# Turning layer 1's softmax shift with one 32-column transpose and eight small DMAs

## The chip, the cores and the metric

The kernel runs on one core of a Trainium2 chip. Its time is the device time of one execution in microseconds (us). The median of three runs counts. One further execution was recorded by the hardware profiler.

## What is computed

Two transformer layers act on `x` of 2048 tokens by 128 channels, each with a modulated layer norm before attention and before a feed-forward part. The change is in the attention of layer 1, which has 8 query heads of 16 channels, one shared key and value head, and a causal mask:

```python
h = _layernorm(x, axis=-1) * (1 + ca) + sa
k = h @ Wk
v = h @ Wv
q = jnp.einsum('btc,qcd->bqtd', h, Wq)
wei = jnp.einsum('bqtd,bsd->bqts', q, k) * scale
wei = jnp.where(causal, wei, -jnp.inf)
wei = jax.nn.softmax(wei, axis=-1)
out = jnp.einsum('bqts,bsd->btqd', wei, v).reshape(b, t, -1)
x = x + ga * (out @ Wp + bp)
```

Layer 0 has attention over all 2048 keys with 16 heads of 8 channels, then a mixture of 16 experts with one chosen per token. Layer 1 ends in a feed-forward part that mixes each token with the one before it.

## The kernel before, in words

One function, `attention`, serves both layers. `fused` is true in layer 0 and false in layer 1. The queries lie in four blocks `b` of 512 (`QB`), the heads in groups `grp` of four. A unit is one pair (b, grp), so layer 1 has eight units, numbered 0 to 7 in the order of blocks: units 0 and 1 belong to block 0, units 6 and 7 to block 3. In layer 1 a unit of block b sees only the keys of blocks 0 to b.

Each unit runs in two passes:

- The first pass (`first_pass`, the step's matmul at L381) computes scores with the queries on the partitions, and VectorE takes the largest per query and head: L385 for whole key blocks, L390 for the block that the mask crosses. Its ending, `largest`, writes the negated maxima into a tile `nm`, as a rounded part (L408) and a remainder (L409).
- The turn (`turn`) brings these maxima from one query per partition to one query per column. TensorE transposes `nm` into a PSUM bank and ScalarE copies the result into a tile `mT`.
- The second pass (`second_pass`) computes the scores again with the keys on the partitions (`score`, L458). In layer 1 a second matmul adds the shift to the same PSUM tile: a matrix of ones against `shift[u]` (L464). ScalarE takes the exponential (L468), GpSimd clears what the mask forbids (L471), and TensorE multiplies by the values (`weigh`, L484).

In layer 0 the shift needs no matmul of its own, because the rows of `mT` are sent by DMA into free rows of the stacked queries `qS` (L424). There `nm` has 32 columns, and one transpose (L417) and one copy of 32 rows (L419) turn it. In layer 1 the shift is a tile `mT` of 128 rows by 512 columns in which, for each of the two row groups of 64, four rows hold numbers and the rest are zero. To get them, `nm` is a zeroed tile of 128 by 512 in which eight columns per 128 are written, and four transposes of 128 by 128 (L431) and a copy of 128 by 512 (L432) turn it.

Three things set the order of the work. First, the program order: `look_ahead` runs the first pass ahead of the second by up to `LEAD` = 8 steps, and calls a unit's `turn` on the third call after its maxima are done. Second, a planner reorders each engine's instructions by its own estimate of when their operands are ready; it may place instructions of different units among each other, on SyncE's queue too. Third, each engine then works strictly in its order. Score tiles of both passes share three PSUM buffers (`ps_s`), and two further banks hold the weighted sums (`av`) and serve everything else (`other_bank`).

The ending of a unit (`normalise`) copies the weighted sum (L554), transposes it back (L522), divides (L526, L527), and after the second group of a block transposes again (L534), copies (L537), projects (L543) and adds to `x` (L550). The queries of block b + 1 are prepared during the first passes of block b: `project_q` splits them and `stack` (L260) sends them by sixteen DMAs of 64 KB, all on SyncE's queue, into `qS`. The next norm's statistics (L180, L181) and the finished rows of the output (L1247) are also made in these gaps.

Of the kernel before, what the change touches and what calls it, by code (L numbers as in the profile page):

```python
# [10 lines left out]
F32 = mybir.dt.float32  # L11
F32R = mybir.dt.float32r
# [7 lines left out]
P = 128  # L20
T = 2048
NT = T // P
QB = 512
NB = T // QB
TB = QB // P
# [9 lines left out]
RT = 64  # L35
# [8 lines left out]
def two_layers(ctx: ExitStack, tc: tile.TileContext, a: dict, out: bass.AP):  # L44
    nc = tc.nc
# [3 lines left out]
    ident = const.tile([P, P], F32, name="ident")  # L49
# [237 lines left out]
    def attention(layer, hT, ngrp, dk, scale, causal, kvp, begin, prepare, wq, bq, folded, ended,  # L287
# [16 lines left out]
        L = f"a{layer}"  # L304
        step = RT // dk
        fused = step > 4
        lag = int(causal)
        S = P // RT
        nst = HG // S
        nrow = S * dk  # L310
        with ExitStack() as s:
            qp = s.enter_context(tc.tile_pool(name=L + "q", bufs=2))
# [9 lines left out]
            def other_bank():  # L322
                nonlocal others
                others += 1
                return banks[(weighing + 1 if fused or weighing >= 0 else others) % 2]
# [4 lines left out]
            qS = {}  # L330
# [4 lines left out]
                ones = kvp.tile([P, nst, P], F32R, name=L + "ones")  # L335
                nc.gpsimd.tensor_copy(ones, ones_rows.unsqueeze(2).to_broadcast([P, nst, P]))
            masked = kvp.tile([P, QB], F32, name=L + "masked") if causal else None
            negmax = []
            for i in range(2):
                shape = [P, nst, TB, S, 2] if fused else [P, TB, P]  # L340
                t = kvp.tile(shape, F32, name=f"{L}nm{i}", tag=f"nm{i}")
                nc.gpsimd.memset(t, 0.0)
                negmax.append(t)

            units = [(b, grp) for b in range(NB) for grp in range(ngrp)]
            attended = {}
# [21 lines left out]
            def first_pass(u):  # L368

                b, grp = units[u]  # L370
                pm = qp.tile([P, TB, HG, NB], F32, name=f"{L}mx{u}", tag="mx")
                nkb = b + 1 if causal else NB

                def step(i, kb, pair):
                    own = causal and kb == b
                    n = (i + 1) * P if own else QB
                    ps = ps_s.tile([P, 2, QB], F32, name=f"{L}p1_{u}_{i}_{kb}_{pair}", tag="s")
                    for j in range(2):
                        g = 2 * pair + j
                        st, r = grp * nst + g // S, RT * (g % S)  # L380
                        nc.tensor.matmul(ps[:, j, :n], qS[b][r:r + RT, st, i * P:(i + 1) * P],  # L381
                                         kS(st)[r:r + RT, kb * QB:kb * QB + n],
                                         start=True, stop=True)
                    if not own:
                        nc.vector.tensor_reduce(pm[:, i, 2 * pair:2 * pair + 2, kb], ps,  # L385
                                                AX.X, ALU.max)
                    for j in range(2 if own else 0):

                        g = 2 * pair + j
                        nc.vector.tensor_tensor_reduce(  # L390
                            masked[:, :n], ps[:, j, :n], later[:, QB - n:], 1.0, LOWEST,
                            ALU.add, ALU.max, pm[:, i, g, kb:kb + 1])

                def largest():
                    nx = qp.tile([P, TB, HG], F32, name=f"{L}nx{u}", tag="nx")
                    nc.vector.tensor_reduce(nx, pm[:, :, :, :nkb], AX.X, ALU.max, negate=True)
                    nm = negmax[u % 2]
                    if fused:


                        parts = [(nm[:, k],
                                  nx[:, :, k * S:(k + 1) * S]) for k in range(nst)]
                    else:

                        parts = [(nm.rearrange("p t (g w) -> p t g w", w=RT)[:, :, :, 2 * k:],
                                  nx[:, :, k * S:(k + 1) * S]) for k in range(nst)]
                    for v, nk in parts:
                        nc.vector.tensor_copy(v[:, :, :, 0].bitcast(F32R), nk)  # L408
                        nc.vector.tensor_tensor(v[:, :, :, 1], nk, v[:, :, :, 0], ALU.subtract)  # L409

                def turn():
                    nm = negmax[u % 2]
                    ps = other_bank()
                    if fused:
                        n = nst * TB * 2 * S
                        mT = qp.tile([n, P], F32R, name=f"{L}mT{u}", tag="mT")
                        nc.tensor.transpose(ps[:n, :P], nm.rearrange("p k t g w -> p (k t g w)"),  # L417
                                            ident)
                        nc.scalar.copy(mT, ps[:n, :P])  # L419

                        for k in reversed(range(nst)):
                            for i in range(TB):
                                r = (k * TB + i) * 2 * S
                                nc.sync.dma_start(  # L424
                                    out=qS[b][31::32, grp * nst + k,
                                              i * P:(i + 1) * P].bitcast(F32),
                                    in_=mT[r:r + 2 * S, :].bitcast(F32))
                    else:
                        mT = qp.tile([P, QB], F32R, name=f"{L}mT{u}", tag="mT")
                        for i in range(TB):  # L430
                            nc.tensor.transpose(ps[:, i * P:(i + 1) * P], nm[:, i, :], ident)  # L431
                        nc.scalar.copy(mT, ps)  # L432
                    shift[u] = mT

                steps = [(lambda i=i, kb=kb, pair=pair: step(i, kb, pair))
                         for i in range(TB) for kb in range(nkb) for pair in range(HG // 2)]
                last = steps.pop()
                return steps + [lambda: (last(), largest(), turns.append([0, turn]))]

            def second_pass(u):  # L440
# [429 lines left out]
    def last0(late, bank, ps_s, ep):  # L870
# [41 lines left out]
        def rows():  # L912
# [8 lines left out]
                lambda: tiles(lambda k: (times(k), down(k))), add]  # L921

    attention(0, hT, H0 // HG, D0, 1.0 / math.sqrt(D0), False, pool, begin0, None, wq0,
              vcol(V_BQ), [], ended0, last0,
              [lambda n=n: clear(n) for n in range((NE + 1) * T // (P * CLEAR))])
# [17 lines left out]
    with ExitStack() as s:  # L943
# [147 lines left out]
        for t in range(NT):  # L1091
            nc.gpsimd.indirect_dma_start(
                out=yx[:, t, :], out_offset=None, in_=a["y_rows"],
# [185 lines left out]
    def last1(late, bank, ps_s, ep):  # L1279
# [9 lines left out]
        def begin():  # L1289
# [8 lines left out]
                       lambda: b.square(nc.vector), lambda: b.value(banks[2], 2)]  # L1298

    attention(1, h2, H1 // HG, D1, float(P) ** -0.5, True, pool1,  # L1300
              lambda ep, pp, stacks: ((lambda st: kS1), (lambda kt, head: vA1[:, kt, :]), qS1),
              ready1, wq1, None, folded1, early, last1)
# [66 lines left out]
```

## Time and profile before

| | before |
|---|---|
| median of three runs | 1236.22 us (1233.09 to 1239.17) |
| profiled execution: own time, span | 1246.91 us, 1245.2 us |
| PE (matmul) busy | 1146.1 us, 92% of the span |
| DVE busy | 953.1 us, 77% |
| ACT busy | 766.6 us, 62% |
| POOL busy | 85.0 us, 7% |
| mean DMA rate | 36 GB/s |

PE is TensorE's matmul, PEld its weight load, DVE VectorE, ACT ScalarE, POOL GpSimd, and SPq the queue from which SyncE issues DMAs. Busy shares are averages over the whole span; the attention of layer 1 is the stretch from about 935 to 1222 us. "Granted clock" is the share of full speed that TensorE was given. In rows of one line the three numbers with slashes are the least, the median and the longest duration in ns, and `out<-in` names what is written and read.

### The profile page before, as it was taken

What the parts mean: (1) busy time and instruction counts of PE and PEld (TensorE: products, weight loads), DVE (VectorE), ACT (ScalarE), POOL (GpSimd) and SP (SyncE); (2) the same over time, 40 slices, a digit from 0 to 9 for tenths busy, and PEclk for the clock granted to TensorE, in tenths of its full rate; (3) what the DMA queues carried; (4) which work ended last, traced back from release to release, by engine and by line L of the source; (5) the groups of instructions that cost most, each with busy time, mean ns of one, the idle gap of its engine ahead of it and who ended that gap; (6) DMA issues with size and microseconds to landing.
All of it is one profiled execution on the core that took longest, in us unless ns stands there. A gap on an engine that the chain in (4) does not pass through costs nothing.

```text
span 1245.2 us, 22565 instructions
## 1 busy us (share of the span) xinstructions
PE 1146.1 (92%) x9216; PEld 519.8 (42%) x9216; DVE 953.1 (77%) x1550; ACT 766.6 (62%) x845; POOL 85.0 (7%) x152
## 2 busy tenths in 40 slices
PE   4579999999999999999999999979858999999995
PEld 2233333334433443343343343447624444444443
DVE  4788898899889889889989883343458688898532
ACT  6107777777777777777777778643323355556763
POOL 2002000000000000000000000320321011100101
PEclk9658999999999999999999999999967789999997
DMA  4841010212220212110000000033210101000000
GB/s 125 113 50 35 2 51 3 70 28 77 70 70 2 69 39 79 56 53 2 1 2 2 2 2 2 20 118 91 64 30 15 35 1 35 1 1 1 2 22 13
DMA packets 63880, 45.23 MB, mean 36 GB/s; under 512 B 7009, under 2 KB 57825, under 8 KB 63265
## 3 DMA queue, kind: packets, MB, share of 16 engines
q1 hardware_dynamic: 61008, 40.37, 13.2%
q10 hardware_dynamic: 1744, 1.32, 0.6%
q0 software_dynamic: 1024, 2.10, 0.6%
q8 instruction: 73, 1.20, 0.4%
q14 instruction: 31, 0.25, 0.1%
HBM read 9.88 MB, written 21.95 MB: 26 GB/s over the span
## 4 chain that ended last, share of the span: by engine, by line
PE 80%; DVE 12%; ACT 4%; DMA 1%; issue 1%; another core or an unknown queue 1%; DVEq 0%; SPq 0%; ACTq 0%; POOLq 0%; POOL 0%
PE a0bank L484 24%; PE a0p L458 17%; PE a0p L381 13%; PE a1bank L484 5%; PE a1p L458 4%; DVE a0mx L385 3%; DVE a1mx L385 3%; PE a1p L381 2%; PE a1p L464 2%; DVE a1masked L390 2%; PE sg L987 2%; ACT a0e L468 1%; PE gu L1039 1%; PE a0bank L522 1%
## 5 line engine op out<-in xcount | busy, mean ns | idle before, releaser
L385 DVE TENSOR_REDUCE a0mx<-a0p 128x2 f32<-128x1024 f32 x512 | 623.9, 1225 | 71.3 <-PE a0p L381 61.4
L468 ACT ACTIVATE a0e<-a0p 128x1024 f32<-128x1024 f32 x512 | 521.8, 1024 | 178.7 <-PE a0p L458 154.1
L484 PE MATMUL a0bank<-a0e,vA 128*32 128x256 f32 x4096 | 333.2, 391 | 1.7 <-ACT a0e L468 1.7
L381 PE MATMUL a0p<-kS,a0qS 64*128 64x512 f32 x1024 | 248.2, 480 | 26.4 <-DVE a0mx L385 13.1
L458 PE MATMUL a0p<-a0qS,kS 64*128 64x512 f32 x1024 | 260.5, 497 | 0.0
L468 ACT ACTIVATE a1e<-a1p 128x1024 f32<-128x1024 f32 (+3 forms) x160 | 143.1, 896 | 109.8 <-PE a1p L464 106.6
L458 PEld LDWEIGHTS a0p<-a0qS,kS 64*128 64x128 f32 x1024 | 97.2, 184 | 204.4 <-issue 132.2
L381 PEld LDWEIGHTS a0p<-kS,a0qS 64*128 64x128 f32 x1024 | 100.2, 192 | 111.4 <-ACT a0e L468 57.1
L484 PEld LDWEIGHTS a0bank<-a0e,vA 128*32 128x32 f32 x4096 | 86.3, 108 | 137.8 <-issue 121.5
L385 DVE TENSOR_REDUCE a1mx<-a1p 128x2 f32<-128x1024 f32 x96 | 115.8, 1221 | 14.5 <-PE a1p L381 13.7
L484 PE MATMUL a1bank<-a1e,vA 128*32 128x256 f32 (+1 forms) x1152 | 97.1, 386 | 0.4 <-POOL a1e L471 0.4
L458 PE MATMUL a1p<-a1qS,kS 64*128 64x512 f32 (+3 forms) x320 | 77.7, 470 | 5.2 <-DVE a1mx L385 3.9
L381 PE MATMUL a1p<-kS,a1qS 64*128 64x512 f32 (+3 forms) x320 | 68.2, 426 | 11.4 <-DVE a1mx L390 5.1
L390 DVE CUSTOM_DVE_ANT_0 a1masked<-a1p,later 128x128 f32<-128x128 f32 (+3 forms) x128 | 62.4, 488 | 10.6 <-PE a1p L381 5.2
L793 POOL DMA_INDIRECT sent<-hs,row_i x16 | 16.0, 999 | 707.6 <-DVE ln11xn L229 684.0
L464 PE MATMUL a1p<-a1mT,a1ones 64*128 64x512 f32 (+3 forms) x320 | 62.5, 379 | 0.0
L458 PEld LDWEIGHTS a1p<-a1qS,kS 64*128 64x128 f32 x320 | 32.0, 191 | 63.8 <-issue 25.5
L381 PEld LDWEIGHTS a1p<-kS,a1qS 64*128 64x128 f32 x320 | 33.1, 201 | 38.5 <-DVE a1mx L390 12.7
L484 PEld LDWEIGHTS a1bank<-a1e,vA 128*32 128x32 f32 x1152 | 25.7, 109 | 42.6 <-issue 35.3
L471 POOL TENSOR_SCALAR_AFFINE_SELECT a1e<-a1e 128x256 f32<-128x256 f32 x64 | 26.0, 407 | 234.7 <-ACT a1e L468 234.7
L464 PEld LDWEIGHTS a1p<-a1mT,a1ones 64*128 64x128 f32 x320 | 32.5, 195 | 1.7 <-issue 1.3
L419 ACT CAST a0mT<-a0bank 32x128 fp32r<-32x128 f32 x16 | 4.0, 253 | 41.2 <-PE a0bank L417 41.2
(384 smaller groups left out, 698.7 us busy)
## 6 DMA issues: line engine op xcount, KB each, us to landing
sent<-blank SPq DMA_DIRECT2D x68, 256.0 KB
kS<-a0qS SPq DMA_DIRECT2D x28, 128.0 KB
a0qS<-a0mT SPq DMA_DIRECT2D x128, 2.0 KB
wgu_sb<-in_gate_up SPq DMA_DIRECT2D x1, 2048.0 KB
a0qS<-a0qh SPq DMA_DIRECT2D x62, 32.0 KB
a0qS<-a0ql SPq DMA_DIRECT2D x62, 32.0 KB
xs<-sent SPq DMA_DIRECT2D x31, 64.0 KB
y_rows<-y SPq DMA_DIRECT2D x7, 256.0 KB
```

The costliest lines, as they stand in the source:

```text
L381: nc.tensor.matmul(ps[:, j, :n], qS[b][r:r + RT, st, i * P:(i + 1) * P], kS(st)[r:r + RT, kb * QB:kb * QB + n], start=True, stop=True)
L385: nc.vector.tensor_reduce(pm[:, i, 2 * pair:2 * pair + 2, kb], ps, AX.X, ALU.max)
L390: nc.vector.tensor_tensor_reduce(masked[:, :n], ps[:, j, :n], later[:, QB - n:], 1.0, LOWEST, ALU.add, ALU.max, pm[:, i, g, kb:kb + 1])
L458: nc.tensor.matmul(ps[:, j, q0:], kS(st)[r:r + RT, kt * P:(kt + 1) * P], qS[b][r:r + RT, st, q0:], start=True, stop=fused)
L464: nc.tensor.matmul(ps[:, j, q0:], ones[r:r + RT, g // S, :], shift[u][r:r + RT, q0:], start=False, stop=True)
L468: nc.scalar.activation(e[:, :, q0:], ps[:, :, q0:], AF.Exp, scale=scale)
L471: nc.gpsimd.affine_select(out=e[:, :, q0:q0 + P], in_=e[:, :, q0:q0 + P], compare_op=ALU.is_ge, fill=0.0, base=0, pattern=[[0, 2], [1, P]] ...
L484: nc.tensor.matmul(av[g * W:(g + 1) * W, c0:c1], vA(kt, grp * HG + g), held[kt, g // 2][:, g % 2, c0:c1], start=(kt == 0 and c0 == 0), sto ...
L522: nc.tensor.transpose(ps[:, i * P:(i + 1) * P], o[:, i * P:(i + 1) * P], ident)
L793: nc.gpsimd.indirect_dma_start(out=sent[t], in_=hs[:, i, :], in_offset=None, out_offset=bass.IndirectOffsetOnAxis(ap=row_i.bitcast(U32)[:, ...
L987: nc.tensor.matmul(ps[:, j, :], w[:, k * P:(k + 1) * P], hT[:, b * QB:(b + 1) * QB], start=True, stop=True)
L1039: nc.tensor.matmul(ps[:, i, :], xsT[q][:, i * P:(i + 1) * P], wgu[:, bass.ds(regs[j], 1), :].rearrange("p a f -> p (a f)"), start=True, st ...
```

## The change

In layer 1 the maxima of every unit but unit 0 now go into a tile `nm` of 32 columns, ordered by row group, query tile, pair and part. The turn of these units is one transpose of 32 columns (now L422) and one copy of 32 rows into `small` (L424). Then eight DMAs of four rows by 128 columns (2 KB each, L433) on SyncE's queue put the rows into one of two tiles `rows_of`, at rows 0 to 3 and 64 to 67. These two tiles take the part of `mT` in turn. The second of them is zeroed once by GpSimd; the first is written whole by unit 0, which keeps the four wide transposes through the tile `wide`. The tiles `nm` are no longer zeroed in either layer, since all their columns are written. Lines after the change stand seven further down from `second_pass` on (L458 is L465, L464 is L471, L484 is L491); the first pass's L381 is L383.

```diff
--- before.py
+++ after.py
@@ -335,12 +335,14 @@
                 ones = kvp.tile([P, nst, P], F32R, name=L + "ones")
                 nc.gpsimd.tensor_copy(ones, ones_rows.unsqueeze(2).to_broadcast([P, nst, P]))
             masked = kvp.tile([P, QB], F32, name=L + "masked") if causal else None
-            negmax = []
-            for i in range(2):
-                shape = [P, nst, TB, S, 2] if fused else [P, TB, P]
-                t = kvp.tile(shape, F32, name=f"{L}nm{i}", tag=f"nm{i}")
-                nc.gpsimd.memset(t, 0.0)
-                negmax.append(t)
+            negmax = [kvp.tile([P, nst, TB, S, 2] if fused else [P, S, TB, nst, 2], F32,
+                               name=f"{L}nm{i}", tag=f"nm{i}") for i in range(2)]
+            if not fused:
+
+                wide = kvp.tile([P, TB, P], F32, name=L + "wide")
+                nc.gpsimd.memset(wide, 0.0)
+                rows_of = [kvp.tile([P, QB], F32R, name=f"{L}rows{i}") for i in range(2)]
+                nc.gpsimd.memset(rows_of[1].bitcast(F32), 0.0)
 
             units = [(b, grp) for b in range(NB) for grp in range(ngrp)]
             attended = {}
@@ -400,9 +402,12 @@
 
                         parts = [(nm[:, k],
                                   nx[:, :, k * S:(k + 1) * S]) for k in range(nst)]
+                    elif u:
+                        parts = [(nm[:, :, :, k].rearrange("p g t w -> p t g w"),
+                                  nx[:, :, k * S:(k + 1) * S]) for k in range(nst)]
                     else:
 
-                        parts = [(nm.rearrange("p t (g w) -> p t g w", w=RT)[:, :, :, 2 * k:],
+                        parts = [(wide.rearrange("p t (g w) -> p t g w", w=RT)[:, :, :, 2 * k:],
                                   nx[:, :, k * S:(k + 1) * S]) for k in range(nst)]
                     for v, nk in parts:
                         nc.vector.tensor_copy(v[:, :, :, 0].bitcast(F32R), nk)
@@ -411,25 +416,27 @@
                 def turn():
                     nm = negmax[u % 2]
                     ps = other_bank()
-                    if fused:
-                        n = nst * TB * 2 * S
-                        mT = qp.tile([n, P], F32R, name=f"{L}mT{u}", tag="mT")
-                        nc.tensor.transpose(ps[:n, :P], nm.rearrange("p k t g w -> p (k t g w)"),
-                                            ident)
-                        nc.scalar.copy(mT, ps[:n, :P])
-
-                        for k in reversed(range(nst)):
+                    n = nst * TB * 2 * S
+                    if fused or u:
+                        small = qp.tile([n, P], F32R, name=f"{L}mT{u}", tag="mT")
+                        nc.tensor.transpose(
+                            ps[:n, :P], nm.rearrange("p a t b w -> p (a t b w)"), ident)
+                        nc.scalar.copy(small, ps[:n, :P])
+                        for c in reversed(range(nst if fused else S)):
                             for i in range(TB):
-                                r = (k * TB + i) * 2 * S
-                                nc.sync.dma_start(
-                                    out=qS[b][31::32, grp * nst + k,
-                                              i * P:(i + 1) * P].bitcast(F32),
-                                    in_=mT[r:r + 2 * S, :].bitcast(F32))
+                                cols = slice(i * P, (i + 1) * P)
+                                r = (c * TB + i) * 4
+                                if fused:
+                                    dst = qS[b][31::32, grp * nst + c, cols]
+                                else:
+                                    dst = rows_of[u % 2][c * RT:c * RT + 4, cols]
+                                nc.sync.dma_start(out=dst.bitcast(F32),
+                                                  in_=small[r:r + 4, :].bitcast(F32))
                     else:
-                        mT = qp.tile([P, QB], F32R, name=f"{L}mT{u}", tag="mT")
                         for i in range(TB):
-                            nc.tensor.transpose(ps[:, i * P:(i + 1) * P], nm[:, i, :], ident)
-                        nc.scalar.copy(mT, ps)
+                            nc.tensor.transpose(ps[:, i * P:(i + 1) * P], wide[:, i, :], ident)
+                        nc.scalar.copy(rows_of[0], ps)
+                    mT = None if fused else rows_of[u % 2]
                     shift[u] = mT
 
                 steps = [(lambda i=i, kb=kb, pair=pair: step(i, kb, pair))
```

## The prediction

> **What bounds the kernel now.** I read the page's busy shares first, then stage windows, then the rows around the "turn" of layer 1, unit by unit. The change touches attention layer 1 only, which runs from about 935 to 1222 us of the 1245.2 us span. In the stage windows (columns: window, its length, then busy us and count for PE, PEld, DVE, ACT, POOL, then granted TensorE clock, DMA share, GB/s):
>
> ```profile
> 1030.00:1045.00 15.00, 13.96 (x134) 6.73 (x134) 14.11 (x29) 6.64 (x9) 2.44 (x6) 1.00 0.01 2
> 1045.00:1061.00 16.00, 15.41 (x133) 7.77 (x132) 13.12 (x25) 10.85 (x14) 0.81 (x2) 1.00 0.26 67
> 1061.00:1077.00 16.00, 14.15 (x132) 6.30 (x131) 15.12 (x51) 9.64 (x10) 0.51 (x2) 1.00 0.00 1
> 1077.00:1100.00 23.00, 22.71 (x217) 10.97 (x216) 19.87 (x32) 13.74 (x17) 2.75 (x7) 1.00 0.01 2
> ```
>
> PE is the bound in most of it (96% and 99% busy in the second and fourth row); DVE leads where a unit's maxima end (14.11 of 15, 15.12 of 16), and ACT never does. So PE time removed counts, and a PE stall counts almost in full. What the change works on:
>
> ```profile
> L431 PE MATMUL a1bank<-ident,a1nm x32: 272/273/477, 935.4 to 1165.3; 128*128 128x128 f32 x32
> ...
> L432 ACT CAST a1mT<-a1bank x8: 581/586/587, 936.6 to 1165.9; 128x512 fp32r<-128x512 f32 x8
> ```
>
> And the form that layer 0 already uses, which layer 1 now gets:
>
> ```profile
> L417 PE MATMUL a0bank<-ident,a0nm x16: 270/284/393, 83.6 to 758.0; 128*32 128x128 f32 x16
> ...
> L419 ACT CAST a0mT<-a0bank x16: 239/254/255, 84.0 to 758.5; 32x128 fp32r<-32x128 f32 x16
> ...
> L424 SPq DMA_DIRECT2D a0qS<-a0mT x128: 497/497/594, 84.3 to 762.7; - x128
> ```
>
> **What it takes away.** Seven units lose three of four transposes each. Four in a row span 0.66 us at full clock (1044.05, below), one 0.27: 0.38 saved; at half clock (unit 2: 978.12 to 979.24) 0.84. Only where nothing else sets the unit's start does this reach the end: units 2, 3, 5, 7 give 0.84 + 3 x 0.38 = 2.0 us. Seven ACT copies get shorter by 586 - 254 = 332 ns (2.3 us), but ACT has at least 30% idle in each window above: worth 0, or 2.3 at most. The DVE writes stay four per unit of 0.17 us, and POOL's two 128x512 memsets (0.52 each) are two again: 0; layer 0 only loses two small memsets, and its PE order is unchanged: 0.
>
> **What it adds.** 7 x 8 = 56 DMAs on SP, and a wait: the first ones-matmul (L464 before, L471 now) of a unit now waits for eight landings instead of one ACT copy. PE works in order, so behind it wait all scores, and through the three PSUM score tiles DVE's maxima and ACT's exponentials. The price of the path is read from layer 0, which has the same eight 2 KB DMAs:
>
> ```profile
> 757.95 0.28 PE L417 MATMUL a0bank<-ident,a0nm 128*32 128x128 f32 x1
> ...
> 758.49 0.24 ACT L419 CAST a0mT<-a0bank 32x128 fp32r<-32x128 f32 x1
> ...
> 758.76 4.47 SPq L424 DMA_DIRECT2D a0qS<-a0mT  x8
> ```
>
> 0.78 us from transpose to end of copy, 4.47 for eight issues, and the last issue (762.73) is followed by its last packet 1.24 us after it began (in the unit before: issue 718.75, packets to 719.99). That is 0.75 + 7 x 0.57 + 1.25 = 6.0 us from the transpose to a ready shift; before it was 1.28. Here a rule speaks against a small number: the Trainium skill, "DMA: Bandwidth & Descriptors", section "Anatomy of one DMA", gives about 2.0 us fixed for a DMA of POOL's path, most of it receipt. By that each stall below grows by 0.75 us; the row is for SP's path and nearer, so I take 1.25 and keep 2.0 for the range.
>
> How long each unit had, from the first transpose to the first L464 of that unit in the trace of before (units 1 to 7): 4.65, 7.78, 11.98, 2.65, 8.44, 3.99, 6.68 us. Units 2, 3, 5, 7 have 0.7 us or more left over 6.0. Units 1, 4 and 6 do not.
>
> The built program shows that PE's order is not the old one: the planner saw the later rows and moved work ahead of the wait. Unit 1: one pair of maxima scores and three weighings (0.9 us) come first; arrival about 953.5 against ready at 947.94 + 6.0 = 953.9: 0.3 us lost. Unit 6: scores and weighings (1.7 us) come first; arrival 1127.4 against 1128.0: 0.6 us.
>
> **Unit 4** is different. SP's order there, of the changed program:
>
> ```
> L433 a1rows0 <- a1mT4   4x128  x4    (half of the shift)
> L260 a1qS3 <- a1qh3, a1ql3  32x512  x16   (queries of the last block)
> L433 a1rows0 <- a1mT4   4x128  x4    (the other half)
> ```
>
> Sixteen query DMAs lie between the halves of the shift, and both halves are needed by the first pair. Before:
>
> ```profile
> 1044.05 0.66 PE L431 MATMUL a1bank<-ident,a1nm 128*128 128x128 f32 x4
> ...
> 1045.76 1.11 SPq L260 DMA_DIRECT2D a1qS<-a1qh  x2
> ...
> 1046.70 0.39 PE L464 MATMUL a1p<-a1mT,a1ones 64*128 64x512 f32 x2
> ...
> 1048.51 0.58 ACT L554 COPY a1o<-a1bank 128x512 f32<-128x512 f32 x1 [0.29 <-PE a1bank L484]
> ...
> 1054.55 1.60 SPq L260 DMA_DIRECT2D a1qS<-a1ql  x2
> ```
>
> The sixteen took 1045.76 to 1056.15, 10.4 us. Ready: 1044.05 + 0.75 + 4 x 0.59 + 10.4 + 3 x 0.57 + 1.25 = 1060.5. PE until then: weighings, two maxima pairs, two scores and the whole ending of unit 3 (transposes 0.66, 0.65, projection 1.16) were moved ahead, 5.8 us of work chained through ACT (0.58 twice) and DVE; from the rows after 1046.7 I get arrival at 1053. After that all three score tiles are held, so nothing else can run: **PE idle from 1053 to 1060.5, 7.5 us**. In lateness: at 1060.5 PE has done what before was done by 1046.7 + 5.8 + 0.4 idle = 1052.9: 7.6 us late.
>
> Restart: three exponentials of 1.02 us must free the tiles one after another, about 1.2 us of PE idle. Given back: DVE has done unit 3's additions and the third norm's statistics (about 5 us) in the gap, so the DVE-bound stretch 1061 to 1077, with 1.85 us of PE idle, turns PE-bound: -1.2.
>
> **The clock.** A stall of this length also costs clock. This trace:
>
> ```profile
> 1009.03:1012.44 3.41, 2.13 (x24) 1.01 (x20) 3.41 (x24) 1.08 (x3) 1.22 (x3) 1.00 0.00 0
> 1012.44:1015.85 3.41, 3.23 (x18) 1.58 (x20) 3.41 (x13) 1.02 (x1) 0.00 (x0) 0.50 0.00 0
> 1015.85:1019.27 3.42, 3.42 (x18) 2.15 (x14) 2.86 (x10) 1.80 (x2) 1.27 (x1) 0.50 0.00 0
> 1019.27:1022.68 3.41, 3.32 (x22) 1.43 (x20) 2.37 (x10) 3.11 (x4) 0.00 (x0) 1.00 0.00 0
> ```
>
> A window at 62% PE busy (its longest gap only 1.45 us) was followed by two at half clock, and full clock came back after one that was 100% busy. The skill ("TensorE: Matmul & The Clock Gate", Part 1) asks for an idle window of about 3.4 us to halve and one busy window to restore. By the skill, the gaps in units 1 and 6 are free and unit 4 pays one window; by the row, half clock in unit 4 lasts until about 1067 (first window 90% busy, second 100%), and even a 1.4 us gap elsewhere could cost two. At half clock four transposes take 1.12 instead of 0.66, so a PE-bound window loses 0.4 of its length: one window 1.4 us, 6.6 us about 2.2 net of the restart's idle. I take the row: +2.2.
>
> **Sum.** -2.0 (transposes) + 0.3 + 0.6 (units 1, 6) + 7.6 + 1.2 - 1.2 + 2.2 (unit 4) = **+8.7 us** on the profiled execution, 1246.91 us (span 1245.2), which lies 10.7 above the median of 1236.22; moved to the median, 1245 us (+0.7%).
>
> **Rivals.**
> A (above), 60%: one long stall in unit 4; +6 to +12, 1242 to 1248.
> B, 22%: the stall is there but half is given back: no halved clock beyond the gap (0 instead of 2.2), restart hidden (0), all 1.85 us of DVE-bound idle recovered: -2.0 + 0.9 + 7.6 - 1.85 = +4.7; with an arrival a little later than 1053, +2. For: units 4 and 5 have DVE at 82 to 95%. Against: from 1077 on PE is at 99%. 1238 to 1242.
> C, 8%, not slower: SP's DMAs land before PE arrives. It decides in unit 4: if the sixteen query issues go out fast, or only after the last four, ready is 1050 and PE arrives at 1053. Then -2.0, and with all of ACT's 2.3 us and the 0.38 of units 1, 4 and 6, -5.4: 1231 to 1235. Against: 1.2 to 1.3 us per two issues in every row of L260, and SP runs in order.
> D, 10%: the gaps in units 1 and 6 each halve the clock for two windows as at 1012 (+2.8 each), and unit 4's half clock lasts longer, as it did from 957.8 to 981.7 (seven windows): +14 to +20, 1250 to 1256.
>
> About 0.5% (6.2 us) is what a measurement of this kernel can tell from no change. Slower by more: most of A (0.54) and D: 0.64. Faster by more: the edge of C, 0.03. Rest 0.33. Range: 1237 to 1253, which leaves out C and the end of D.
>
> **What would show it.** Right: eight SP rows per unit from unit 1, split four, sixteen, four around the query DMAs near 1045; the first L471 of unit 4 about 16 us after its transpose; a PE gap of 7 to 8 us there, ended by a DMA, with granted clock 0.5 after it; no PE gap over 1 us at units 2, 3, 5, 7; the L422 group with x7 more rows of about 0.28 us. Wrong: that gap under 4 us (B or C), full clock in 1060 to 1067 (no +2.2), or new gaps over 2 us in other units (D).

## The result, and the profile after

The changed kernel takes 1252.69 us (median of 4 runs, 1249.05 to 1255.44) against 1237.43 us for the kernel before (4 runs, 1233.09 to 1239.17): a ratio of 1.0118, 95% interval 1.0091 to 1.0145, or 15.3 us more. The forecast was 1245 us with a range to 1253: slower, as forecast, by nearly twice the forecast 8.7 us. The profiled execution took 1254.3 us. From its page: the span, the chain that ended last by engine, and the group of the ones-matmul (columns: busy us, mean ns of one, idle of the engine just before, and what ended it). The last row is the same group in the page of before.

```profile
span 1252.6 us, 22627 instructions
...
PE 82%; DVE 9%; ACT 4%; DMA 2%; SPq 2%; issue 1%; POOL 0%; DVEq 0%; ACTq 0%; POOLq 0%
...
L471 PE MATMUL a1p<-a1rows,a1ones 64*128 64x512 f32 (+3 forms) x320 | 64.6, 390 | 10.8 <-DMA a1rows<-a1mT 10.8
...
L464 PE MATMUL a1p<-a1mT,a1ones 64*128 64x512 f32 (+3 forms) x320 | 62.5, 379 | 0.0
```

The last two rows have most of the story: PE stood idle 10.8 us ahead of the ones-matmuls, and what ended that idle time was the DMA of the shift rows. Before, PE did not wait there at all. SyncE's part of the chain (SPq), 2% now, was 0% before. The four stage windows that the prediction showed of before, now of after (unit 4's turn stands at 1037.43 us here, 6.6 us earlier than in that trace):

```profile
1030.00:1045.00 15.00, 12.99 (x118) 6.58 (x114) 14.22 (x32) 5.01 (x9) 2.82 (x7) 1.00 0.09 24
1045.00:1061.00 16.00, 8.41 (x36) 5.08 (x38) 6.72 (x33) 3.88 (x4) 0.00 (x0) 0.52 0.18 46
1061.00:1077.00 16.00, 16.00 (x152) 6.67 (x148) 12.31 (x17) 10.64 (x11) 0.00 (x0) 0.95 0.01 2
1077.00:1100.00 23.00, 22.19 (x215) 10.68 (x207) 20.14 (x39) 14.15 (x18) 3.25 (x8) 1.00 0.01 2
```

In the second window PE is busy 8.41 of 16 us where it was 15.41, and the granted clock is 0.52 where it was 1.00. The reason is in SyncE's timeline (start, us, engine, line):

```profile
1038.03 2.59 SPq L433 DMA_DIRECT2D a1rows<-a1mT  x4
1040.72 1.14 SPq L260 DMA_DIRECT2D a1qS<-a1qh  x2
...
1049.53 1.23 SPq L260 DMA_DIRECT2D a1qS<-a1ql  x2
1050.81 2.52 SPq L433 DMA_DIRECT2D a1rows<-a1mT  x4
```

and its effect in PE's and ACT's:

```profile
1054.50 1.85 PE L471 MATMUL a1p<-a1rows,a1ones 64*128 64x512 f32 x6 [6.94 <-DMA a1rows<-a1mT]
...
1055.59 2.85 ACT L475 ACTIVATE a1e<-a1p 128x1024 f32<-128x1024 f32 x3 [10.67 <-PE a1p L471]
```

Four issues, sixteen of the next queries, four issues: the second half of unit 4's shift goes out 10.2 us after the first half is done, PE waits 6.94 us for it, and ACT 10.67 us for PE.

**Stage by stage.** The time from the turn (first transpose) of one unit to that of the next holds everything that a late shift of that unit costs. The first trace of before spans 7.1 us more than a second one (the run before_again below), and 5.3 us of that lie ahead of the turn of unit 1; the second trace is the yardstick here.

| stage | before | after | difference | forecast for that unit |
|---|---|---|---|---|
| turn 0 to 1 | 12.62 | 13.33 | +0.71 | 0 |
| 1 to 2 | 30.08 | 29.96 | -0.12 | +0.3 |
| 2 to 3 | 23.21 | 23.95 | +0.74 | -0.84 |
| 3 to 4 | 41.60 | 41.37 | -0.23 | -0.38 |
| 4 to 5 | 32.82 | 44.21 | +11.39 | +9.8 |
| 5 to 6 | 45.16 | 44.98 | -0.18 | -0.38 |
| 6 to 7 | 42.88 | 45.12 | +2.24 | +0.6 |
| 7 to the end | 79.65 | 80.83 | +1.18 | -0.38 |
| sum | 308.0 | 323.7 | +15.7 | +8.7 |

The sum agrees with the 15.3 us of the medians, but not as a proof: against the first trace of before it is 14.0, and the first two stages differ between executions with the half clock of their time, whatever the form (e10 below, in the old form, took 13.38 and 27.07 us). For the two stages that carry it, the windows from turn to turn (columns as above), before (second trace) and then after:

```profile
1037.58:1070.40 32.82, 30.44 (x269) 14.71 (x268) 29.18 (x78) 20.74 (x23) 1.22 (x3) 1.00 0.13 33
1115.55:1158.43 42.88, 41.49 (x387) 19.61 (x386) 36.43 (x80) 27.94 (x30) 1.22 (x3) 1.00 0.01 2
```

```profile
1037.43:1081.64 44.21, 34.71 (x265) 16.67 (x265) 30.34 (x78) 20.08 (x23) 1.22 (x3) 0.81 0.10 25
1126.62:1171.74 45.12, 42.85 (x384) 19.76 (x383) 36.33 (x80) 27.55 (x30) 1.22 (x3) 1.00 0.01 2
```

In unit 4's stage PE is busy 4.27 us longer and idle 7.12 us longer (9.50 against 2.38). The longer busy time, though four matmuls fewer are recorded (three of them are the transposes saved), goes with the mean clock of 0.81. In unit 6's stage the clock stayed full: 0.88 us more idle, and 1.36 us more busy. That second part was in no step of the forecast. Nearly half of it shows in the weighings, before (second trace) and after:

```profile
L484 PE MATMUL a1bank<-a1e,vA 128*32 128x256 f32 x191 | 15.7, 391 | 0.0
...
L491 PE MATMUL a1bank<-a1e,vA 128*32 128x256 f32 x191 | 16.3, 391 | 0.0
```

The same number, each of the same length, takes 0.6 us more in all, so they overlap less. The order of PE's work there differs from before; that this is the reason was not tested.

### The profile page after: what moved, and what is told of

It is laid out like the page before. It is cut to its first block, busy times and chain, and to the rows that moved or that the text cites. A ratio compares the mean times of both kernels' runs of the same rounds, so it can differ in the third digit from the quotient of the medians.

```text
span 1252.6 us, 22627 instructions
## 1 busy us (share of the span) xinstructions
PE 1157.3 (92%) x9195; PEld 524.9 (42%) x9195; DVE 954.6 (76%) x1550; ACT 764.7 (61%) x845; POOL 84.6 (7%) x150
## 3 DMA queue, kind: packets, MB, share of 16 engines
q10 hardware_dynamic: 1744, 1.32, 0.6%
q8 instruction: 72, 1.18, 0.4%
## 4 chain that ended last, share of the span: by engine, by line
PE 82%; DVE 9%; ACT 4%; DMA 2%; SPq 2%; issue 1%; POOL 0%; DVEq 0%; ACTq 0%; POOLq 0%
PE a0bank L491 24%; PE a0p L465 17%; PE a0p L383 13%; PE a1bank L491 5%; PE a1p L465 4%; DVE a0mx L387 3%; PE a1p L383 3%; PE a1p L471 2%; PE sg L994 2%; DVE a1masked L392 2%; ACT a0e L475 1%; DVE a1mx L387 1%; PE gu L1046 1%; PE a0bank L529 1%; ACT a1e L475 1%
## 5 line engine op out<-in xcount | busy, mean ns | idle before, releaser
L491 PE MATMUL a0bank<-a0e,vA 128*32 128x256 f32 x4096 | 333.4, 392 | 0.8 <-ACT a0e L475 0.8
L383 PE MATMUL a0p<-kS,a0qS 64*128 64x512 f32 x1024 | 248.1, 480 | 25.5 <-DVE a0mx L387 13.4
L465 PE MATMUL a0p<-a0qS,kS 64*128 64x512 f32 x1024 | 261.1, 499 | 0.0
L465 PEld LDWEIGHTS a0p<-a0qS,kS 64*128 64x128 f32 x1024 | 97.4, 184 | 204.2 <-issue 129.7
L383 PEld LDWEIGHTS a0p<-kS,a0qS 64*128 64x128 f32 x1024 | 100.5, 193 | 110.3 <-ACT a0e L475 57.5
L491 PEld LDWEIGHTS a0bank<-a0e,vA 128*32 128x32 f32 x4096 | 86.6, 109 | 136.8 <-issue 121.9
L491 PE MATMUL a1bank<-a1e,vA 128*32 128x256 f32 (+1 forms) x1152 | 99.5, 391 | 0.4 <-POOL a1e L478 0.4
L465 PE MATMUL a1p<-a1qS,kS 64*128 64x512 f32 (+3 forms) x320 | 78.9, 476 | 3.9 <-DVE a1mx L387 2.3
L383 PE MATMUL a1p<-kS,a1qS 64*128 64x512 f32 (+3 forms) x320 | 73.2, 439 | 8.5 <-DVE a1mx L392 4.2
L471 PE MATMUL a1p<-a1rows,a1ones 64*128 64x512 f32 (+3 forms) x320 | 64.6, 390 | 10.8 <-DMA a1rows<-a1mT 10.8
L800 POOL DMA_INDIRECT sent<-hs,row_i x16 | 15.7, 984 | 708.0 <-DVE ln11xn L229 684.2
L465 PEld LDWEIGHTS a1p<-a1qS,kS 64*128 64x128 f32 x320 | 32.3, 192 | 64.8 <-issue 29.9
L383 PEld LDWEIGHTS a1p<-kS,a1qS 64*128 64x128 f32 x320 | 35.2, 205 | 36.6 <-ACT a1e L475 13.3
L491 PEld LDWEIGHTS a1bank<-a1e,vA 128*32 128x32 f32 x1152 | 26.1, 110 | 42.8 <-issue 35.6
L471 PEld LDWEIGHTS a1p<-a1rows,a1ones 64*128 64x128 f32 x320 | 34.4, 200 | 13.4 <-issue 12.7
L424 ACT CAST a0mT<-a0bank 32x128 fp32r<-32x128 f32 x16 | 4.0, 253 | 40.7 <-PE a0bank L422 40.7
```

Of the source, the lines that this page charges most:

```text
L465: nc.tensor.matmul(ps[:, j, q0:], kS(st)[r:r + RT, kt * P:(kt + 1) * P], qS[b][r:r + RT, st, q0:], start=True, stop=fused)
L471: nc.tensor.matmul(ps[:, j, q0:], ones[r:r + RT, g // S, :], shift[u][r:r + RT, q0:], start=False, stop=True)
L491: nc.tensor.matmul(av[g * W:(g + 1) * W, c0:c1], vA(kt, grp * HG + g), held[kt, g // 2][:, g % 2, c0:c1], start=(kt == 0 and c0 == 0), sto ...
L800: nc.gpsimd.indirect_dma_start(out=sent[t], in_=hs[:, i, :], in_offset=None, out_offset=bass.IndirectOffsetOnAxis(ap=row_i.bitcast(U32)[:, ...
```

## The experiments

Every kernel was compared with the kernel before on the same chip. Chips differ (medians of before from 1237 to 1248 us), so only ratios are carried from one to another; the microseconds behind a ratio are the ratio less 1, times that chip's median of before.

**The change again.** This is the changed kernel as it stands.

> The change itself, timed again beside the other variants on one chip, so that its size can be set against theirs. Theory (the stall of unit 4 and its restart are nearly all of it): 1.010 to 1.014 of the kernel before, and in the trace about 11 us more between the turns of units 4 and 5, 2 us more between those of 6 and 7, nothing elsewhere. Rival (the size differs from execution to execution with the granted clock): the ratio moves to 1.006 or 1.018 while the gap in unit 4 stays near 7 us.

Measured: ratio 1.0127 (1.0103 to 1.0152), +15.8 us; stages 4 to 5 and 6 to 7 at 43.77 and 45.95 us, that is +10.95 and +3.07. The size holds. What differs from the first trace is the clock: in unit 6's stage there was one window at half clock (1141.7 to 1145.1 us) where the first trace had none.

**Unit 4 left in the old form** (e1_unit4_wide).

```diff
-                    elif u:
+                    elif u not in (0, 4):
...
-                    if fused or u:
+                    if fused or u not in (0, 4):
...
-                        nc.scalar.copy(rows_of[0], ps)
+                        nc.scalar.copy(rows_of[u % 2], ps)
```

> The change in units 1, 2, 3, 5, 6 and 7; unit 4 keeps its four wide transposes and the wide copy. Theory: nearly all of the +15 us (profile: +11.4 between the turns of units 4 and 5) is unit 4's shift, whose second half stands behind sixteen query DMAs on SyncE's queue. Then this kernel is +1 to +4 us over before: the PE gaps of 1.1 to 1.4 us at units 1, 6 and 7 stay, the rest is gone, the turn of unit 5 follows that of unit 4 by about 33 us as before, not 44. Rival 1 (the eight small DMAs and the wait for them cost each of the seven units alike, some 2.2 us): six sevenths remain, +13 us.

Measured: 1.0036 (1.0022 to 1.0050), +4.5 us. Unit 4's stage is as before, 32.78 us with the clock full:

```profile
1045.91:1078.69 32.78, 30.36 (x269) 14.70 (x268) 29.14 (x78) 20.77 (x23) 1.22 (x3) 1.00 0.13 33
```

So unit 4 is worth 15.8 - 4.5 = 11.3 us, and 4.5 us come from the other six units, which the forecast had at -1.1 in sum. In the trace they show PE gaps of 1.52, 1.32 and 1.35 us ahead of the first ones-matmul of units 1, 6 and 7.

**Unit 4 alone in the new form** (e2_only_unit4; the same edit with `u == 4`).

> The change in unit 4 alone; all other units keep the wide turn. Theory: +10 to +13 us over before, with one PE gap of about 7 us before the first L471 of unit 4, about 17 us after its transpose, and half clock around it. Rival 1 (a like cost in each unit): +2 us. Rival 2 (the cost is in the planner's other order of PE around units 1, 2 and 6): 0 us.

Measured: 1.0072 (1.0046 to 1.0097), +9.0 us (5.7 to 12.1); a gap of 7.92 us, stage 4 to 5 at 44.01 us, no other gap at a turn. The forecast's 9.8 us for this unit lies inside.

**SyncE's order: the queries behind the shift** (e3_queries_later). The call that projects the next block's queries moves from the start of the first pass of unit 4 to the fifth step of the first pass of unit 5 (in block 1 from unit 2 to unit 3), so that SyncE issues the eight shift DMAs first and then the sixteen.

```diff
-                            ready.insert(len(ready) - 1, lambda b=b: project_q(b + 1))
+                            if b == 0:
+                                ready.insert(len(ready) - 1, lambda b=b: project_q(b + 1))
+                        if not fused and (grp, i) == (1, 4) and 0 < b < NB - 1:
+                            project_q(b + 1)
```

> The changed kernel, with the queries of blocks 2 and 3 prepared in the first pass of the block's second unit instead of its first, so that on SyncE's queue the eight shift DMAs of unit 4 stand ahead of the sixteen query DMAs. Nothing else is moved. Theory: unit 4's shift is ready about 6.5 to 7 us after its transpose instead of 17, the PE gap there falls from 6.9 to under 2 us, the time to +1 to +5 us over before. Rival 1 (the wait for eight DMAs as such): +13 to +15 us. If the queries' new place costs, unit 3 or 5 shows a new gap.

SyncE's and PE's timeline of it:

```profile
1044.50 5.09 SPq L433 DMA_DIRECT2D a1rows<-a1mT  x8
1049.70 1.14 SPq L260 DMA_DIRECT2D a1qS<-a1qh  x2
```

```profile
1050.78 0.70 PE L471 MATMUL a1p<-a1rows,a1ones 64*128 64x512 f32 x2 [0.31 <-DMA a1rows<-a1mT]
```

The shift comes in 6.88 us after its transpose in place of 17.07, and the gap shrinks from 6.94 to 0.31 us. That the split makes the stall is shown. The time, though, came out at 1.0084 (1.0053 to 1.0116), with runs from 1252 to 1265 us. It was timed again:

> The sixteen query DMAs behind the shift DMAs, timed again: the first timing gave 1.0084 while its own profile had lost nearly the whole stall (turn of unit 1 to end 2.6 us over before). Theory X (the order costs little, the first timing was widened by executions with a longer stretch of half clock): 1.001 to 1.005, and the trace again 2 to 4 us over before from the turn of unit 1. Theory Y (the late queries make a new wait that the first profile missed, or that stands in another block): 1.007 or more again, and the trace shows a PE gap of several us ended by a query DMA, or more time between two turns than in the first profile.

Measured: 1.0064 (1.0042 to 1.0087), +8.0 us, between the two theories. The trace has no gap ended by a query DMA; from the turn of unit 0 to the end it shows 5.2 us over before (second trace) in the first profile and 6.7 in the second. Units 1, 6 and 7 keep their gaps (about 4.5 us by e1), and stages 3 to 4 and 4 to 5 together are about 1.0 us longer (39.74 + 35.63 against 41.60 + 32.82). Some 2.5 us of the 8 stay unexplained; the two profiled executions show part of them at most.

**Does a split hurt any unit?** (e6_only_235; new form for `u in (2, 3, 5)`.) The planner then happens to split unit 2's shift instead.

> The new turn in units 2, 3 and 5 alone, the old one elsewhere. In the built order SP now splits unit 2's shift: six of its DMAs, then the sixteen query DMAs of block 2, then the last two. Theory (a split by query DMAs makes the stall, whichever unit it hits): unit 2 is ready about 17 us after its transpose against 8 without the split, so PE waits about 8 us there: +7 to +11 us, 1.006 to 1.009, and unit 4 has no gap. Rival (the stall belongs to unit 4, and units 2, 3, 5 are the ones that gain): 0.998 to 1.000.

```profile
980.86 4.02 SPq L433 DMA_DIRECT2D a1rows<-a1mT  x6
...
995.60 1.27 SPq L433 DMA_DIRECT2D a1rows<-a1mT  x2
```

```profile
998.04 1.85 PE L471 MATMUL a1p<-a1rows,a1ones 64*128 64x512 f32 x6 [5.48 <-DMA a1rows<-a1mT]
```

Measured: 1.0066 (1.0046 to 1.0086), +8.2 us. Unit 2, which had no gap in the change, now waits 5.48 us, its shift arriving 17.90 us after its transpose, and its stage takes 34.08 us against 23.21. Unit 4, in the old form, has none. The stall follows the split, not the unit.

**Another queue** (e7_act_queue): layer 1's shift DMAs on ScalarE's queue.

```diff
-                                nc.sync.dma_start(out=dst.bitcast(F32),
-                                                  in_=small[r:r + 4, :].bitcast(F32))
+                                (nc.sync if fused else nc.scalar).dma_start(
+                                    out=dst.bitcast(F32), in_=small[r:r + 4, :].bitcast(F32))
```

> Layer 1's shift DMAs are issued by ScalarE in place of SyncE, so that they don't stand in one queue with the query DMAs. Theory (SyncE's order makes the stall): unit 4's gap is under 2 us, the time between the turns of units 4 and 5 is 33 to 35 us, and what is left is +1 to +5 us for the eight issues on ScalarE's queue ahead of its exponentials, 0.999 to 1.005. Rival (the transfers themselves are slowed by 16 query transfers of 64 KB in flight): unit 4 still waits more than 5 us for its last shift DMA and the ratio stays above 1.008.

Measured: 1.0186 (1.0154 to 1.0218), +23 us: the slowest of all. PE has no gap at a turn any more, and unit 4's stage is down to 37.11 us, so the rival (slow transfers) is out, though SyncE issued the sixteen query DMAs from 1046.20 us on beside them; but my price for ScalarE was far too low. Its timeline at unit 4:

```profile
1044.46 5.09 ACTq L433 DMA_DIRECT2D a1rows<-a1mT  x8
...
1049.65 0.66 ACT L475 ACTIVATE a1e<-a1p 128x256 f32<-128x256 f32 x2 [5.22 <-DMA a1rows<-a1mT]
```

While ScalarE issues eight DMAs it computes no exponential: the first one behind them waits 5.22 us, though its scores were in the bank by 1044.5. The score tiles are not freed and PE waits for ACT instead. The wait moved from PE to ScalarE: in this trace its exponentials wait for the shift DMAs five times, 26.1 us in all, and the last stage alone is 85.14 us against 79.65. (This trace is the fastest of the kernel's six runs.)

**Filling the gap** (e5_repeat_projection): the block-1 projection's four products are made six times over into the same bank, so that PE works through part of the stall.

```diff
-                    for i in range(TB):
+                    for i in [i for _ in range(6 if causal and b == 1 else 1) for i in range(TB)]:
```

> The changed kernel, in which the projection of block 1 (four matmuls that end just before unit 4's wait) is computed six times over into the same bank, which fills the 6.9 us gap with about 6 us of PE work of no use. It prices the clock. Theory (the halved clock from 1045.7 to 1062.7 is a cost of its own): the first L471 of unit 4 still comes about 17 us after its transpose, but clock is full when it comes, and the stretch from there to the turn of unit 5 is 2 to 4 us shorter than the 27.1 us of the changed kernel; in time +11 to +13 us over before. Rival 3 (the clock costs nothing there, since PE waits for ACT and DVE at the restart anyway): same as the changed kernel, +15 us or more.

```profile
1057.76 2.40 PE L550 MATMUL a1bank<-a1wog,a1onT 128*128 128x128 f32 x20
1063.44 1.85 PE L471 MATMUL a1p<-a1rows,a1ones 64*128 64x512 f32 x6 [3.29 <-DMA a1rows<-a1mT]
```

Measured: 1.0114 (1.0083 to 1.0144), not to be told from the change. The half clock lasted 6.8 us in all instead of 17.1 and 13.7 in the two traces of the change, but 6.5 us of it (against 8.2 in the first trace of after and 7.3 in the second) still fell on the work behind the stall, and the stage took 43.46 us (44.21 and 43.77). The expectation was wrong: the clock was not full when the ones-matmul came, and from there to the turn of unit 5 it is 26.4 us against 27.1, not 2 to 4 us less. By these three executions the half clock behind the stall costs about 0.4 us for each us, and filling half of the gap hardly moved that. A kernel with a long stall and no half clock behind it was not made.

**The small gaps by themselves**, beside a second trace of before.

> The kernel before itself, for a trace of it from the same chip as the other variants, since the first trace of it is one execution on another chip, with a time 10.7 us over the median it stands beside. If that trace stands for the kernel, the turn of unit 1 to the end is 296 to 299 us again, with no PE gap over 1 us at a unit's first ones-matmul; if not, 292 us or less, and each comparison with it has to be moved by the difference.

Measured: ratio 0.9995 (0.9979 to 1.0010). Turn of unit 1 to the end: 295.40 us, just under what the expectation gave and 1.9 under the first trace; no gap at a turn. What else the first trace had more lay ahead of that turn.

e9_only_167 has the new form for `u in (1, 6, 7)` alone.

> The new turn in units 1, 6 and 7 alone, the three in which the change's trace has a gap of 1.1 to 1.4 us ahead of the first ones-matmul; SyncE issues all eight DMAs of each in one run. Theory (small gaps cost their length, the restart and a window of half clock now and then): +3 to +7 us, 1.0025 to 1.0055, with gaps of 1.1 to 1.5 us at the three units and 2 to 3 us more from the turn of unit 6 to that of unit 7. Rival (as the prediction had it, such gaps are worth 0.3 and 0.6 us): 0.999 to 1.001.

Measured: 1.0041 (1.0024 to 1.0058), +5.1 us (3.0 to 7.2). These three units were +0.5 us in the forecast (0.3 + 0.6 - 0.38). Gaps 1.39, 1.38 and 1.09 us. Around unit 6's gap, which ends at 1120.70:

```profile
1116.80:1120.60 3.80, 2.48 (x22) 0.87 (x20) 2.31 (x10) 0.58 (x1) 0.00 (x0) 1.00 0.01 3
1120.60:1124.00 3.40, 3.30 (x12) 2.17 (x14) 1.23 (x1) 1.94 (x2) 0.00 (x0) 0.50 0.03 5
1124.00:1127.40 3.40, 3.40 (x20) 1.38 (x18) 2.29 (x2) 2.05 (x2) 0.00 (x0) 0.50 0.00 0
```

A gap of 1.38 us, in a window in which PE was 65% busy, and then two windows at half clock in which 12 and 20 matmuls are recorded where a full one has about 30. The stage took 47.00 us. Put beside the other traces, stage 6 to 7 falls into three groups: no half window behind the gap, 45.08, 45.10 and 45.12 us (e5, the first e3, after); one, 45.80, 45.95 and 45.96 (e1, after_again, e3_queries_again); two, 47.00 (e9). A half window costs 0.7 to 0.95 us there, and the rest, 2.2 us over the 42.88 of before, is there with the clock full. The last stage falls apart in the same way: 80.72 to 80.95 us without a half window behind unit 7's gap (after, e1, second e3, e5, e9), 82.21 and 82.26 with one (after_again, first e3).

**A version meant to beat both** (e8_235_queries_later): the new form in units 2, 3 and 5, with the edit of e3 so that no shift is split.

> A version meant to beat both: the new turn in units 2, 3 and 5 alone, which have 7.8 to 12 us from transpose to use, the old one in units 1, 4, 6 and 7, and the projection of the next block's queries placed behind those units' shift DMAs so that SyncE splits none of them. Theory: no wait is left, three transposes are saved in each of three units (0.84 + 0.38 + 0.38 = 1.6 us), and it is 0.998 to 1.000. Rival (the later queries cost something themselves): 1.002 to 1.006, with longer stages in blocks 1 and 2 but no PE gap at a first ones-matmul.

Measured: 0.9989 (0.9976 to 1.0001), -1.4 us (-3.0 to +0.1); unit 2's eight DMAs go out in one run, and no gap is left at a first ones-matmul. Its control has only the moved projection, in the kernel before:

> The kernel before with only the projection of the next block's queries moved later, as in the version with the new turn in units 2, 3 and 5, which came out at 0.9989 with 2.1 us less from the turn of unit 0 to the end. If those 2 us are the saved transposes (1.6 us), this kernel is within 0.5 us of before, 0.9995 to 1.0005; if they come from the moved projection, it is 1.5 to 2.5 us faster by itself, 0.998 to 0.999. In the trace: the stage from the turn of unit 3 to that of unit 4 about 1.6 us shorter and the next one as much longer, in both cases.

Measured: 0.9999 (0.9983 to 1.0015). Stage 3 to 4 is 1.1 us shorter than in before (40.49) and stage 4 to 5 1.8 longer (34.58). So the moved projection by itself is worth nothing that shows. The 1.4 us would fit the saved transposes (1.6), but both intervals hold 1, and the traces don't bear it out: the stages of units 2, 3 and 5 take 108.42 us together in e8 and 108.22 in e10, which has the old form. That the new form gains in its three good units is not shown.

## Why the prediction was right or wrong

**Mechanism and place: right; the size: too small.** Rival A's story is what happened: the 4, 16, 4 order, a first ones-matmul 17.07 us after its transpose (16.4 was worked out), a gap of 6.94 us (7.5), half clock until 25.3 us after the transpose (about 23), no gap at units 2, 3 and 5. But +15.3 us lies in rival D's span (+14 to +20) and not in A's (+6 to +12), and the median lies 0.3 us inside the range, with two of the four runs above it: that the range held is luck. The L422 row for layer 1 has the seven short transposes:

```profile
L422 PE MATMUL a1bank<-ident,a1nm x7: 284/285/397, 942.2 to 1171.7; 128*32 128x128 f32 x7
```

**Unit 4's sum: right in size.** 9.8 us forecast; 11.4 in the stage, 11.3 by difference (the change less e1), 9.0 alone (e2). In idle time, against the second trace of before: 1.39 us ahead of the gap (0.17 before), 6.94 in it, 0.66 in the six us behind it (0.41), 0.52 from there to the next turn (1.80). That is +7.12 for 7.6 + 1.2 - 1.2: the 1.2 given back is there (1.28), the restart cost about 0.25 and not 1.2, and the gap is near 7.5 in part by luck, since PE came to it 10.1 us after the transpose (9.0 forecast) and the shift 17.07 (16.4). What was mis-sized is the clock: +4.27 us busy for 2.2. The stretch at half clock in after and in after_again:

```profile
1045.67:1062.73 17.06, 9.47 (x46) 4.94 (x44) 7.73 (x34) 4.90 (x5) 0.00 (x0) 0.50 0.16 40
1056.35:1070.01 13.66, 6.62 (x32) 3.45 (x36) 5.58 (x31) 4.31 (x5) 0.00 (x0) 0.50 0.12 31
```

PE worked 9.47 us of it in after, 6.62 in after_again and 6.76 in e2, and the stage's busy time grew by 4.27, 2.99 and 3.06: 0.45 us for each us at half clock, three times over. In after the clock fell at 1045.67, before the gap opened at 1047.56; the window before was 73% busy.

**The path of 6.0 us: the step that failed.** It is 6.88 us in unit 6. Worked out from that unit's rows (transpose 1126.62, eight issues from 1127.22 to 1132.31, ones-matmul 1133.50): 0.60 to the first issue (0.75 forecast), 4.51 from first issue to last (3.99), 1.77 from the last issue to PE (1.25). One reason for the middle term is that the same 2 KB take longer to issue into layer 1's tiles than into layer 0's:

```profile
L433 SPq DMA_DIRECT2D a0qS<-a0mT x128: 497/497/591, 85.5 to 764.2; - x128
...
L433 SPq DMA_DIRECT2D a1rows<-a1mT x56: 577/577/717, 943.1 to 1177.6; - x56
```

The last term was read from the end of the last packet, and PE does not go on then: the last packet of unit 6's shift ends at 1133.06, and PE starts 0.44 us later. With the 2.0 us that the Trainium skill ("DMA: Bandwidth & Descriptors", "Anatomy of one DMA") states for POOL's path, and that the prediction set aside for the nearer row, the path would have been 6.75; the measured 1.77 lies between the two, nearer to the page.

**What hung on it.** In units 1, 6 and 7 PE arrived 5.83, 5.57 and 6.46 us after the transpose, much as forecast (5.6, 5.4 and 6.7), but the shift came at 7.22, 6.88 and 7.58 in place of 6.0. So 0.3, 0.6 and "0.7 us left over" became gaps of 1.39, 1.31 and 1.12. The line "no PE gap over 1 us at units 2, 3, 5, 7" was wrong for unit 7.

**The price of a small gap: wrong too.** The forecast charged its length only. Unit 6's 1.31 us cost 2.2 us with the clock full, 3.1 with one half window behind it and 4.1 with two. Together the three units are +5.1 us (e9) where the sum had +0.5: this is most of the 6.6 us by which the forecast fell short. Part of it is rival D's mechanism, with 1.9 us for two half windows in place of 2.8, and in some executions only. The Trainium skill ("TensorE: Matmul & The Clock Gate", Part 1) has the clock fall after an idle window of about 3.4 us; here a 1.38 us gap was enough in e9, and a 1.31 us gap was not in after. The page also says that the window runs freely, not from the kernel's start. The traces agree so far: in each, the changes of the clock lie whole multiples of 3.41 us apart, and the gap falls in another part of that grid from run to run. The window around the gap in after, then the one in after_again and the one behind it:

```profile
1131.00:1134.41 3.41, 2.10 (x22) 1.04 (x16) 1.19 (x3) 0.70 (x2) 0.00 (x0) 1.00 0.02 5
...
1138.27:1141.69 3.42, 2.10 (x21) 0.92 (x23) 1.68 (x5) 0.59 (x1) 0.00 (x0) 1.00 0.02 5
1141.69:1145.10 3.41, 3.41 (x16) 2.06 (x16) 1.23 (x1) 2.17 (x3) 0.00 (x0) 0.50 0.02 5
```

On this grid PE was busy 52, 61, 61 and 62% of the window in the four traces in which half clock followed (second e3, e1, after_again, e9), and 62, 63 and 67% in the three in which it did not (after, e5, first e3, where the gap is shared with a window that is 78% busy). So unit 6's gap lies on the edge; no kernel here moved it on purpose, and why e9 paid two windows stays open.

**The savings:** -2.0 was forecast for units 2, 3, 5 and 7. Units 3 and 5 show -0.23 and -0.18 in their stages (-0.38 each); unit 7 lost; unit 2's stage differs by more than its saving between executions of one form (22.37 to 23.21 us in the old one, 22.65 to 23.95 in the new one with the queries in their old place) and shows nothing. Its 0.84 was too large in any case: it takes one transpose at full clock from four at half, and one at half clock takes 0.40 us (the longest of the seven above), which leaves 0.72. Rival B (half given back) is out by its own sign, a gap under 4 us; rival C's condition (the queries only after the last four) was made in e3, and it removed the stall but did not make the kernel faster: the small gaps stay (about 4.5 of the 8.0 us), and some 2.5 us are unexplained.

## What to carry to other kernels

A small DMA that a matmul waits for must be looked up in the order of its queue, not only in its own cost: a planner that put sixteen large issues between two small ones turned a 7 us path into 17. Read such a path from first instruction to the waiting engine's restart in a place where that engine does wait, since issue rows and packet ends leave out the last half microsecond. And slack alone doesn't say where such a change is free: units 2, 3 and 5 had 7.8 us and more from transpose to use, but with the new form in these three alone the planner split unit 2's shift, and the kernel was 8.2 us slower. With the order mended as well, nothing was lost (-1.4 us, -3.0 to +0.1), and a gain is not shown.

## What the runs showed of the hardware

- A PE gap of 1.3 to 1.4 us ahead of unit 6's ones-matmul was followed by no window of 3.4 us at half clock in three traces, by one in three and by two in one; two executions of the changed kernel differ in this. A half window cost 0.7 to 0.95 us in that stage.
- In unit 4's stage PE's busy time grew by 0.45 us for each us that it worked at half clock (9.47, 6.62 and 6.76 us in three traces).
- The same 2 KB DMA took SyncE 497 ns into one tile and 577 ns into another, and ScalarE 585 ns; on ScalarE the eight issues took 5.1 us, in which it made no exponential. From the last packet's end to the restart of the waiting PE it was 0.44 us.
- With full clock, PE was busy 1.36 us longer in unit 6's stage, with three transposes fewer and the work in another order.
